# Layer 0 of a four-layer image network: another written-out order of its steps

## The chip, the cores and the metric

The kernel runs on one core of one Trainium2 chip. The metric is the device time of one execution in microseconds (us). Three runs of the kernel before took 6542.04, 6547.03 and 6561.65 us; their median, 6547.03 us, is the time that the prediction is held against. The core has a matrix engine (TensorE, called PE in the profile, with its weight loads as PEld), a vector engine (VectorE, DVE), a scalar engine for activations (ScalarE, ACT), a general engine (GpSimd, POOL), and a queue that issues transfers (SyncE, SP). Each engine runs its own list of instructions in order and waits where it needs a result of another.

## The reference

A batch of 32 images with 96 channels of 56x56 passes through four layers. Each layer is `x = x + layer(group_norm(x))`, with groups of three channels. Only layer 0 is touched by the change:

```python
h = einsum('nchw,oc->nohw', xn, w_exp)          # 96 -> 576 channels
h = silu(bn1(h))
h = depthwise_conv3x3(h, w_dw)                  # one 3x3 filter per channel
h = silu(bn2(h))
s = sigmoid(silu(h.mean((2, 3)) @ w_se1.T) @ w_se2.T)   # a gate per image and channel
h = einsum('nchw,oc->nohw', h * s[:, :, None, None], w_proj)   # 576 -> 96
out = bn3(h) + xn                               # and x + out outside
```

Layers 1 to 3 (a wavelet convolution, a quantised block of the same shape as layer 0, and a 9x9 convolution) follow one after the other.

## The kernel before, in words

**Tiling.** Layer 0 handles one image after the other. The 576 middle channels are cut into five blocks of 128 (the last is 64 channels, held twice). Blocks 0 and 1 have their 3x3 filters on VectorE, nine taps each; the upper half of block 2 is filtered on VectorE too; the lower half of block 2, all of block 3 and all of block 4 are filtered on TensorE, as matrix products with diagonal 32x32 weights.

**The steps.** A step has a letter, and its digits are its arguments: `e` (`expand`) multiplies one row tile of one block and lets ScalarE write it into a padded buffer (`e40` is block 4, tile 0); `f` (`first_tap`, ScalarE) and `t` (`tap`, VectorE) filter blocks 0 to 2 (`t18` is block 1, tap 8); `x0`, `a0`, `a1` and `c0` are the four filter groups on TensorE, each a call of `parts` with 9 taps x 4 x 4 small products on 32x32 parts of the array; `z` (`end_block`, ScalarE) ends a block; `g0` to `g4` make the gate (totals, squeeze, excite, gates, gated weights); `p` (`project`) multiplies one tile down to 96 channels; `d` (`add`, VectorE) adds it to the image; `o` (`store`) takes the statistics for the next layer and issues the stores; `s u m q v w b n r` are the group norm and the residual.

**Order.** `L0_ORDER` (line 61) is the list of the steps of one iteration n, and `run_steps` (line 116) goes through it once for each image. `-` after a step means image n-1 and `+` image n+1, so three images are in work at once. TensorE, VectorE and ScalarE keep the order of this list (line 473), each its own steps of it; the queue SP isn't among them, and has its transfers in the order in which they are written, each starting when what it waits for is done.

**Stores.** Two images share a buffer of the pool `pairs`, of which there are two. `store` of an odd image (line 453) issues six stores of the pair, 392 KB each and one per 16 channels (line 162), then the load of the pair after the next into the same buffer (`fetch(b + 3)`, line 211), and then some small copies for later layers (`aside`, lines 552 and 579).

**Buffers.** All products land in tiles of one PSUM pool with four buffers, taken in turn. A filter group takes two of them and gives them back after four ScalarE instructions. The normalised image `xn` has one buffer. Blocks 0, 1 and 2 share two padded buffers, block 3 and block 4 have one each.

Of the kernel before, what the change touches and what calls it, by code (L numbers as in the profile page):

```python
# [58 lines left out]
MANUAL = {mybir.EngineType.PE, mybir.EngineType.DVE, mybir.EngineType.Activation}  # L59
MANUAL_SP = MANUAL | {mybir.EngineType.SP}  # L60
L0_ORDER = """
    g2- g3- e40 t01 g4- e12 t02 t03 e30 t04 e41 e13 p0- d0- p1- s+ u+ t05 p2- m+ r t06 d1- t07 d2-
    p3- q+ f1 t08 e42 d3- e31 e32 e33 e20 v+ e21 o- w+ t11 e22 e23 t12 b+ e43 f2 t13 t14 t21 t15 z0
    x0 t16 a0 t22 t17 t18 n+ c0 t23 z1 t24 t25 t26 a1 t27 e00+ t28 z2 e01+ e02+ g0 e03+ g1 f0+ e10+
    e11+
"""
L2_ORDER = """
    e00 e10 e11 e12 l3 j0- d0- e01 e20 e02 e21 r u+ e03 e13 j1- m0 e22 d1- e30 m1 e40 v+ j2- d2- e31
# [1334 lines left out]
```

## Time and profile before

The profile is of one execution that took 6533.3 us; the span from its first to its last instruction is 6531.3 us. It is 13.7 us below the median of the runs.

| what | value | where it stands |
|---|---|---|
| median of the runs | 6547.03 us | times |
| profiled execution, span | 6533.3 us, 6531.3 us | times, page |
| TensorE busy | 5997.0 us, 92% | page, part 1 |
| VectorE busy | 4809.6 us, 74% | page, part 1 |
| ScalarE busy | 3988.3 us, 61% | page, part 1 |
| mean granted TensorE clock | 0.959 | clock of the core |
| filter groups of layer 0 on TensorE (line 376) | 875.6 us + 315.8 us busy | page, part 5 |
| idle before them, mostly for "issue" | 122.9 us + 110.0 us | page, part 5 |

In a profile a line such as `L376 PE MATMUL psd<-hpad,diag` means: line 376 of the kernel, on TensorE, matrix products that read the tiles hpad and diag and write psd. What stands behind "idle before" is how long the engine had nothing running before instructions of this group, and what ended that. "Issue" means that nothing in the profile was being waited for. The chain of waits goes back from the last instruction, at each step to what released it. A timeline lists one engine's instructions in order: start, length, what, and in brackets the idle time before.

The steps of layer 0 stand between about 30 us and 3,390 us of the span.

### The profile page before, as it was taken

The page shows a single profiled execution, that of the slowest core. Times are in us where ns is not written, and L with a number is a line of the kernel's source. Part 1 is how long each engine was busy: PE and PEld are TensorE (multiplying, and loading weights), DVE is VectorE, ACT ScalarE, POOL GpSimd, SP SyncE. Part 2 cuts the span into 40 slices and gives each one's busy share as a digit, 9 for nine tenths or more (in the row PEclk, how much of TensorE's full clock was granted, in tenths as well). Part 3 has the DMA queues.
Part 4 walks back from the last instruction along what each step waited for, and adds up shares of the span by engine and source line. Part 5 has one row for each costly group of instructions (what it writes and reads, how often), then busy time and mean ns, then how long its engine had stood idle before and what let it go on. Part 6 is the DMA issues. An engine that isn't in the chain of part 4 may idle for free.

```text
span 6531.3 us, 163776 instructions
## 1 busy us (share of the span) xinstructions
PE 5997.0 (92%) x72872; PEld 3871.0 (59%) x72872; DVE 4809.6 (74%) x5766; ACT 3988.3 (61%) x5716; POOL 230.5 (4%) x157
## 2 busy tenths in 40 slices
PE   6899999989899989998979999989899999999799
PEld 4555555555555555555545666668777777777344
DVE  7877778777787878777756766657677776676587
ACT  5566565655666565665635656657676776666455
POOL 4000000000000000000000000000000000000000
PEclk8999999999999999999989999989999999999899
DMA  3202221122212222122144676665869696962988
GB/s 99 34 22 53 53 44 32 41 55 49 41 27 47 54 46 41 26 48 41 17 48 134 148 141 158 148 47 38 52 39 53 40 54 40 52 37 30 167 257 243
DMA packets 1305952, 456.47 MB, mean 70 GB/s; under 512 B 1123150, under 2 KB 1301062, under 8 KB 1303326
## 3 DMA queue, kind: packets, MB, share of 16 engines
q1 hardware_dynamic: 1305246, 446.00, 45.6%
q8 instruction: 572, 9.37, 0.6%
q14 instruction: 134, 1.10, 0.1%
HBM read 284.90 MB, written 214.08 MB: 76 GB/s over the span
## 4 chain that ended last, share of the span: by engine, by line
PE 77%; DVE 9%; ACT 7%; issue 5%; DMA 1%; SPq 1%; POOL 0%; ACTq 0%; DVEq 0%
PE ps L329 11%; PE psd L376 11%; PE psd L1051 11%; PE psj L438 7%; PE ps L1032 6%; PE pc L1203 6%; PE pc L767 6%; DVE h L354 6%; PE psj L1088 3%; DVE h2c L354 3%; PE psj L442 3%; PE psj L443 3%; ACT hi L1004 2%; PE pc L751 2%; ACT a L1022 2%
## 5 line engine op out<-in xcount | busy, mean ns | idle before, releaser
L354 DVE SCALAR_TENSOR_TENSOR h<-hpad,l_wdw,h 128x3136 f32<-128x3136 f32 x512 | 1780.7, 3478 | 8.6 <-ACT h L349 1.7
L1051 PE MATMUL psd<-apad,diag 64*64 64x392 bf16 x20736 | 929.9, 331 | 117.2 <-issue 62.7
L376 PE MATMUL psd<-hpad,diag 32*32 32x392 f32 x27648 | 875.6, 543 | 122.9 <-issue 122.6
L329 PE MATMUL ps<-xn,l_wexp 96*128 96x392 f32 x2560 | 961.6, 533 | 16.7 <-DVE nm L296 6.2
L1051 PEld LDWEIGHTS <-diag 64*64 64x64 bf16 x20736 | 692.7, 107 | 350.2 <-issue 171.7
L376 PEld LDWEIGHTS psd<-hpad,diag 32*32 32x32 f32 x27648 | 556.8, 105 | 412.2 <-issue 267.2
L329 PEld LDWEIGHTS ps<-xn,l_wexp 96*128 96x128 f32 x2560 | 513.1, 205 | 405.4 <-issue 96.2
L597 ACT COPY T<-raw 32x112 f32<-32x112 f32 (+2 forms) x1440 | 462.8, 384 | 290.3 <-DMA raw<-tdiff 192.5
L1022 ACT ACTIVATE u<-ps,o,s 128x784 int16<-128x784 f32 x576 | 536.8, 1003 | 160.7 <-PE ps L1032 141.8
L1022 ACT ACTIVATE a<-psd,o,s 128x784 int16<-128x784 f32 x448 | 424.2, 1000 | 332.2 <-PE psd L1051 332.0
L341 ACT ACTIVATE hpad<-ps,o,s 128x784 f32<-128x784 f32 x512 | 537.3, 1071 | 82.5 <-PE ps L329 81.5
L354 DVE SCALAR_TENSOR_TENSOR h2c<-hpad,l_wdw,h2c 128x1568 f32<-128x1568 f32 x256 | 473.5, 1850 | 6.1 <-ACT h2c L349 0.4
L1032 PE MATMUL ps<-hi,l_w1q 96*128 96x392 f32 x1280 | 462.5, 361 | 9.3 <-ACT hi L1004 9.2
L1203 PE MATMUL pc<-x,T 128*112 128x416 f32 (+1 forms) x1152 | 414.8, 523 | 37.0 <-DMA X<-y 37.0
L767 PE MATMUL pc<-x,T 128*112 128x416 f32 (+1 forms) x1152 | 446.0, 523 | 0.0
L1032 PE MATMUL ps<-lo,l_w1q 96*128 96x392 f32 x1280 | 438.1, 342 | 0.0
L376 PE MATMUL psd<-hhalf,diag 32*32 32x392 f32 x9216 | 315.8, 555 | 110.0 <-issue 110.0
L360 ACT ACTIVATE hab<-psd,o,s 128x392 f32<-128x392 f32 x256 | 170.3, 674 | 396.8 <-PE psd L376 396.8
L438 PE MATMUL psj<-h,wg 128*96 128x392 f32 x1024 | 397.9, 509 | 2.3 <-DVE wg L429 2.3
L1203 PEld LDWEIGHTS pc<-x,T 128*112 128x112 f32 x1152 | 204.7, 178 | 246.6 <-issue 233.3
L349 ACT ACTIVATE h<-hpad,l_wdw 128x3136 f32<-128x3136 f32 x64 | 186.2, 2910 | 247.1 <-PE psj L438 247.1
L376 PEld LDWEIGHTS psd<-hhalf,diag 32*32 32x32 f32 x9216 | 191.7, 106 | 205.7 <-issue 158.5
(219 smaller groups left out, 8237.0 us busy)
## 6 DMA issues: line engine op xcount, KB each, us to landing
X<-y SPq DMA_DIRECT2D x192, 392.0 KB
y<-xt SPq DMA_DIRECT2D x180, 392.0 KB
xt<-in_x_dram SPq DMA_DIRECT2D x16, 2352.0 KB
y<-y SPq DMA_DIRECT2D x96, 392.0 KB
xt<-y SPq DMA_DIRECT2D x96, 392.0 KB
out_dram<-y SPq DMA_DIRECT2D x96, 392.0 KB
twav<-zwav SPq DMA_DIRECT2D x768, 36.8 KB
raw<-twav SPq DMA_DIRECT2D x96, 168.0 KB
```

Source lines behind the costliest of these rows:

```text
L329: nc.tensor.matmul(ps[:, j, :NT], wexp[:, k * 128 : k * 128 + 128], im["xn"][:, j, rows, :].rearrange("c h w -> c (h w)"), start=True, sto ...
L341: nc.scalar.activation(window(im["pad"][k][p], p.stop - (p.start or 0), 0, 0, r0, n).rearrange("p r (w j) -> p j r w", j=2), ps[p, :, :NT] ...
L354: nc.vector.scalar_tensor_tensor(h2, window(im["pad"][k], 128, t // 3 - 1, t % 3 - 1, 0, h2.shape[1]), wdw[:, k, t : t + 1], h2, ALU.mult, ...
L376: nc.tensor.matmul(ps[s // 2][q, s % 2, :NT].rearrange("p (r w) -> p r w", w=W2), diag[p, k - XX, t, :], v[:, :, s % 2 : W : 2], start=(t ...
L438: nc.tensor.matmul(out.rearrange("c (r w) -> c r w", w=W2), wg[:, k, :], im["h2"][k][:, rows, j::2], start=(k == 0), stop=False)
L442: nc.tensor.matmul(out, wg[:, COL[AB] + s, :], hab[:, i, j], start=False, stop=False)
L597: nc.scalar.copy(to.rearrange("x t (p s) -> x t p s", p=NPH), v[:, k])
L767: nc.tensor.matmul(ps[:PH, to], st["T"][j][:, h, k, :], st["x"][:, j, h, of], start=False, stop=(n == NK - 1))
L1022: nc.scalar.activation(out, ps, AF.Identity, bias=o[:, c : c + 1], scale=s[:, c : c + 1])
L1032: nc.tensor.matmul(ps[:, j, :NT], w1[:, k * 128 : k * 128 + 128], im[part][:, r0 : r0 + RT, :].rearrange("c h w -> c (h w)"), start=(part ...
L1051: nc.tensor.matmul(ps[q, j, :NT].rearrange("p (r w) -> p r w", w=W), diag[p, k, t, :], v, start=(t == 0), stop=(t == 8))
L1203: nc.tensor.matmul(ps[:, :, to], st["T"][:, h, k, :], st["x"][:, h, :, of], start=(n == 0), stop=(n == NK - 1))
```

## The change

`L0_ORDER` alone changes. The list has the same 77 steps; `e11`, `e30`, `e31` and `e32` change the iteration in which they stand: `e11` from the end of iteration n-1 to the start of iteration n, the other three from iteration n to the end of iteration n-1. So each image still runs the same instructions, with other neighbours.

```diff
 L0_ORDER = """
-    g2- g3- e40 t01 g4- e12 t02 t03 e30 t04 e41 e13 p0- d0- p1- s+ u+ t05 p2- m+ r t06 d1- t07 d2-
-    p3- q+ f1 t08 e42 d3- e31 e32 e33 e20 v+ e21 o- w+ t11 e22 e23 t12 b+ e43 f2 t13 t14 t21 t15 z0
-    x0 t16 a0 t22 t17 t18 n+ c0 t23 z1 t24 t25 t26 a1 t27 e00+ t28 z2 e01+ e02+ g0 e03+ g1 f0+ e10+
-    e11+
+    e11 g2- g3- t01 e40 g4- e12 t02 e33 e13 s+ p0- t03 p1- t04 p2- p3- d0- t05 r u+ d1- t06 t07 d2-
+    d3- m+ t08 f1 q+ t11 t12 a0 e41 e42 e20 t13 e21 e43 e22 t14 v+ w+ t15 t16 b+ t17 e23 f2 z0 c0
+    n+ t21 x0 t18 z1 a1 o- t22 t23 t24 e00+ t25 e01+ t26 e30+ t27 t28 e02+ e03+ e31+ z2 e32+
+    e10+ g0 g1 f0+
 """
```

On TensorE alone the two lists read, one iteration long:

```
before: g2- e40 e12 e30 e41 e13 p0- p1- u+ p2- p3- e42 e31 e32 e33 e20 v+ e21 e22 e23 e43 x0 a0 c0 a1
        e00+ e01+ e02+ e03+ g1 e10+ e11+
after:  e11 g2- e40 e12 e33 e13 p0- p1- p2- p3- u+ a0 e41 e42 e20 e21 e43 e22 v+ e23 c0 x0 a1
        e00+ e01+ e30+ e02+ e03+ e31+ e32+ e10+ g1
```

On VectorE the statistics of `o-` move from right behind `d3-` to behind `t18`, and block 1's taps stand ahead of the half block's.

## The prediction

> **What bounds the kernel now.** I read the page's busy shares first.
>
> ```profile
> PE 5997.0 (92%) x72872; PEld 3871.0 (59%) x72872; DVE 4809.6 (74%) x5766; ACT 3988.3 (61%) x5716; POOL 230.5 (4%) x157
> ```
>
> TensorE leads. Next I took the starts of the statistics of each image (line 88) in the timeline as marks, one per iteration, and the busy times between them. The columns are the stretch, its length, and busy us of PE, PEld, DVE, ACT and POOL, the clock, DMA share and GB/s.
>
> ```profile
> 1008.50:1103.70 95.20, 94.49 (x1366) 55.94 (x1365) 81.53 (x60) 63.19 (x76) 3.63 (x1) 0.96 0.06 15
> 1103.70:1216.90 113.20, 100.41 (x1366) 56.19 (x1365) 81.55 (x61) 63.00 (x76) 3.63 (x1) 0.91 0.36 68
> ```
>
> The same 1366 products take 95.2 us and then 113.2 us, all through layer 0: the 15 long stretches have a mean of 112.3, the 15 short ones 95.2. The long one has the DMA traffic. TensorE sets the time of both; VectorE's 81.5 us fit into either. The chain of waits shows where the 18 us go:
>
> ```profile
> 1117.55 3.93 PE psd L376 x113
> 1121.48 1.46 issue
> 1122.94 3.88 PE psd L376 x121
> 1126.82 2.61 issue
> 1129.43 5.19 PE psd L376 x124
> 1134.61 2.04 issue
> ```
>
> Filter groups come in bursts with holes in which nothing is waited for. TensorE's timeline gives such a burst its full count:
>
> ```profile
> 1122.94 3.88 PE L376 MATMUL psd<-hpad,diag 32*32 32x392 f32 x128 [1.46 <-issue]
> ```
>
> 128 products and their 128 weight loads are 256 instructions: one block of instructions, used up in 3.8 us, and then a wait for the next. The queue called "instruction" moves 16 KB pieces; in the long stretches these start at about 14.3, 21, 28, 34.5, 41, 49.5 and 54 us after the pair's first store. SP's queue:
>
> ```profile
> 1100.02 34.49 SPq L162 DMA_DIRECT2D y<-xt  x6
> ...
> 1142.97 0.34 SPq L211 DMA_DIRECT2D xt<-in_x_dram  x1
> ```
>
> The stores run from 0 to 42 us after that mark and the load of the next pair from 43 to 56, so one instruction block gets through per store (6.5 us), one during the load. Without stores the four groups took 33.3 us (1015.24 to 1048.5, 8.3 each); here 51.9.
>
> **What starts the stores.** In layer 0 the last add `d3-` and the statistics are neighbours; layer 2 has the same store function with work between them:
>
> ```profile
> 4774.85 1.15 DVE L1095 SCALAR_TENSOR_TENSOR xt<-psj,s,xt 96x392 f32<-96x392 f32 x2
> 4777.50 0.98 DVE L1041 TENSOR_SCALAR apad<-u 128x3136 bf16<-128x3136 int16 x1 [1.50 <-ACT u L1022]
> 4778.39 1.96 DVE L87 BATCH_NORM_STATS2 sth<-xt 96x6 f32<-96x392 f32 x4
> ```
>
> and, on SP,
>
> ```profile
> 4776.03 34.53 SPq L162 DMA_DIRECT2D y<-xt  x6
> ```
>
> The store starts 0.03 us after the last add ends (4776.00) and 2.4 us ahead of the statistics. So it follows `d3-`, wherever `o-` stands.
>
> [...] here the first hole comes after 170 to 240 products of a group, so the trace speaks for two blocks. [...] Here half-clock pieces of 3.4 or 6.8 us stand in most short stretches about 52 us in, right behind the squeeze and excite products: a mean loss of 3.4 us by the trace's record of the clock.
>
> **The change, part by part.** Nothing is added or removed: the same 77 steps, transfers included. Three things move.
>
> *(1) The undisturbed iteration.* Durations from the stretch at 1003 to 1099: expand tile 1.32 us (20 products in 6.59), project tile 6.78 (27.1 for four), excite 2.97, squeeze 0.66, tap 3.48, half tap 1.87, add 1.40, statistics 4.2, group eviction 2.7. I count from the end of `t28`. `z2` on ScalarE ends at 1.9, totals at 2.25, squeeze at 2.95; behind two evictions of 1.0 the squeeze's activation is done at 4.15; excite at 7.1, the gate's adds at 7.4, `t01` at 10.8, gated weights at 12.4. TensorE fills 7.1 to 12.4 with `e40 e12 e33 e13`, projects until 39.5; `d3-` ends at 40.9. From there VectorE runs without a wait: `t08` 3.45, `t11`-`t14` 13.9, `t15`-`t17` 10.4, `t21` 1.8, `t18` 3.4, `o-` 4.2, seven half taps 13.1, small ones 0.5: 50.7, so the next `t28` ends at 91.6. TensorE: `a0` 8.3, seven expands and `v+` 9.4, three groups 25.0, eight expands 10.6: 92.8, which is 1.2 before the totals release the squeeze. The iteration is 91.6, plus 3.4 of half clock 95.0, against 95.2. No gain, no loss. The cover is thin: VectorE and TensorE have 1 to 2 us to spare at `p0`, `d3-` and `g1`. Of what is queued behind new waits: PSUM tiles for `a0` need `d1-` and `d2-`, done at 37.5, 2 us early; ScalarE, where `f1` waits for `p3-` with `q+` and `a0`'s evictions behind it, is free at 45.5 and `a0` ends at 47.9; `n+` needs `b+` at 65.8 and gets its turn at 68.4. `e11` at the front is evicted at 8.3, before its buffer is needed. `o-` ends at 78.8, 38 us after the stores' start, before they end, so the load of the next pair (it overwrites what `o-` reads) isn't held.
>
> *(2) The storing iteration (15 of them).* In the new order stores start at `d3-`, 1.4 us after `a0` begins. After the mark at 40.9: `a0` from -1.4 to 6.9, `c0 x0 a1` from 16.5 to 41.5 if undisturbed. Both are in the window of 0 to 56; before, the groups stood at 10.5 to 43.8, undisturbed. I count blocks: a group needs 576 instructions, 2.25 blocks of 3.7 us; half a block and a full one are at hand at a start after slow work; the next are usable about 1.7 us after the starts above (16, 22.7, 29.5, 36, 42.7, 52.5, then free). Before, nine blocks from 10.5: 1.5 at hand, holes at 19.7, 26.4, 33.2, 39.7 and 46.4, end 61.8; the trace has 62.4, a loss of 18.0. After: `a0` has 1.5 of its 2.25 at hand and the third was asked for at about 0.5, before the queues fill: done at 7. While seven expands run (70 instructions in 9.2 us), the next block comes in. `c0` then starts at 16.5 with 1.5 blocks, gets a block at 22.7, and needs the next at 26, 33, 40 and 46; they come at 29.5, 36, 42.7 and 52.5: 6.75 blocks end at 56 to 57, a loss of 15.6. If `a0` asks later than 1 us, it waits for the turn at 7.5 and ends at 10 to 11; if `c0` then misses the turn at 21, the end is 60 to 61, a loss of 19.6. The phase of the block at the start decides, and the counts don't fix it. The first case gives 18.0 - 15.8 = 2.2 us per storing iteration, 33 us over 15; the second costs 1.6, 24 us.
>
> *(3) Squeeze and excite* have one expand tile between them, not two, and a wait of 1.2 us ahead. [...] short stretches lose 0 to 6.8 us now. I take +0.3 us for 31 iterations, 9 us; none as the low end, 3.4 in every second iteration, 53 us, as the high.
>
> Sum: -33 + 9 = -24 on the profiled 6533.3 us, 6509; the median is 13.7 above that execution, so 6523 us. Filling the pipeline differs too (three expands earlier, `e11` later), by a few us at one iteration in 33, either way; I leave it out.
>
> **The rivals.** *Even out* (6550 us): half of the storing iterations miss a turn, (-2.2 + 1.6) / 2 x 15 = -5, with the 9 us above +4. For it: four groups in the window now, where the last one used to run half outside it; against: two starts with full blocks, not one. *Slower* (6600 us): the half-clock piece of (3). No gain from blocks and 3.4 us in every second iteration is +53. It decides from six extra pieces of 6.8 us on (20 us). For it: 3 of 15 short stretches already have 13.7 us at half clock; [...] *The store is held back to `o-`* (6285 us): then the window would open behind `a1` and close before the next `a0`, and 15 x 17.5 = 262 us would go. Layer 2's start, 0.03 us behind the add, speaks against it.
>
> **How the numbers follow.** 0.3% of the time, 20 us, is what a measurement tells from none (the three runs lie 20 us apart). The gain by blocks has 0.37, evening out 0.33, slower 0.26, the held store 0.04. Faster is 0.37 + 0.04 = 0.41, same 0.33, slower 0.26. The likeliest case's own range is 6490 to 6527; the range with the others goes from 6470 (one hole of about 5 us less in each storing iteration, 75 us, and no extra half clock) to 6590, and leaves out the held store and the end of the slower case.
>
> **What would show it.** Right: long stretches of about 110.5, short of 95; stores starting within 0.1 us of `d3-`; in the storing iterations `a0` with at most one hole, and holes in `x0` and `a1`, with the end of `a1` 57 to 58 us after the first store. Wrong: long stretches below 105 (the stores start later, or blocks come faster), an end of `a1` past 61, half-clock pieces in more places than behind the excite, or TensorE waiting over 2 us for the totals or for gated weights in short stretches, which would make (1) wrong.

## The result and the profile after

The changed kernel takes 6571.55 us (median of 12 runs, 6548.36 to 6588.71) beside 6549.6 us of the kernel before in the same 12 rounds (6527.86 to 6582.35). The ratio is 1.0024, 95% interval [1.0005, 1.0043]. The forecast was 24 us faster. By the ratio it came out about 16 us slower, by the medians 22. That is about the 20 us (0.3%) that the prediction took for no change, but the interval leaves 1 out: there is a small loss and not a gain. The profiled execution took 6588.7 us, its span is 6586.6 us, the mean granted clock is 0.951 (0.959 before).

The two profiled executions are 55 us apart while the medians differ by 22: that of before lies 16 us below its median of 12, that of after 17 above. A second profile of the changed kernel is used below. Of the kernel before there is only the one, so differences to it are uncertain by its 16 us; the timed runs, split by their clocks under "The sum again", settle what the profiles can't.

From the page of the kernel after, part 1 and the groups of layer 0 on TensorE (busy time and mean ns | idle before, and what ended it):

```profile
PE 6061.0 (92%) x72872; PEld 3877.2 (59%) x72872; DVE 4807.8 (73%) x5766; ACT 3976.9 (60%) x5716; POOL 244.2 (4%) x157
...
L376 PE MATMUL psd<-hpad,diag 32*32 32x392 f32 x27648 | 898.3, 557 | 178.9 <-issue 175.2
...
L329 PE MATMUL ps<-xn,l_wexp 96*128 96x392 f32 x2560 | 986.8, 544 | 36.6 <-ACT hab L360 22.6
...
L376 PE MATMUL psd<-hhalf,diag 32*32 32x392 f32 x9216 | 291.7, 523 | 25.7 <-issue 24.9
```

The holes ahead of the filter groups fell from 122.9 + 110.0 = 232.9 us to 178.9 + 25.7 = 204.6: 28 us less, near the 33 us of the forecast. But the same instructions got longer: TensorE's busy time rose by 64.0 us, of which 25.2 are the expand tiles' (961.6 to 986.8). Most of this is a lower clock: by the trace's record of it, half clock took 267 us of the span before and 320 after. And a new wait of 22.6 us for `hab` stands in the list, once in the whole run.

To place these I cut both traces at the first projection `p0-` of each iteration. The columns are as in the prediction: stretch, length, busy PE, PEld, DVE, ACT, POOL, clock, DMA share, GB/s. Before, the start and one short and one long iteration:

```profile
0.00:146.60 146.60, 94.73 (x1332) 59.65 (x1333) 105.74 (x298) 87.91 (x97) 76.29 (x60) 0.88 0.39 106
976.00:1071.20 95.20, 94.49 (x1365) 55.96 (x1364) 82.89 (x62) 63.13 (x77) 3.63 (x1) 0.96 0.10 31
1071.20:1184.40 113.20, 100.41 (x1366) 56.18 (x1365) 81.07 (x61) 63.06 (x77) 3.63 (x1) 0.91 0.33 56
```

After:

```profile
0.00:163.30 163.30, 96.43 (x1340) 57.59 (x1341) 106.00 (x298) 89.83 (x99) 88.16 (x60) 0.83 0.36 97
996.90:1092.30 95.40, 95.16 (x1365) 56.88 (x1364) 82.38 (x61) 62.66 (x76) 3.69 (x1) 0.96 0.10 30
1092.30:1208.50 116.20, 102.35 (x1366) 58.54 (x1365) 81.54 (x61) 62.96 (x77) 3.63 (x1) 0.90 0.33 56
```

Three readings. The start is 16.7 us longer. The short iteration is the same. The storing iteration is longer at a lower clock. Over the 14 storing and 14 other iterations of images 1 to 28 (worked out from the trace; "half-clock loss" is half of the time that TensorE spent at half clock, idle or busy):

| kernel | storing: length | holes in groups | half-clock loss | other: length | half-clock loss | first projection at | last projection's start |
|---|---|---|---|---|---|---|---|
| before | 112.75 | 15.05 | 7.31 | 95.23 | 3.41 | 146.6 | 3353.6 |
| after | 114.36 | 13.44 | 9.87 | 95.76 | 3.66 | 163.3 | 3403.0 |
| after, second profile | 114.00 | 13.49 | 9.14 | 95.16 | 3.41 | 163.9 | 3387.8 |

So both profiles agree: holes fall by 1.6 us in each storing iteration, half-clock loss rises by 1.8 to 2.6 in the same iterations, and the iteration becomes 1.3 to 1.6 us longer than in the one profile of before, instead of 2.2 shorter. Behind layer 0 the rest of the span is 3177.7 us before, 3183.6 and 3189.1 after; with the same instructions there, this is scatter.

**What starts the stores, and what a late `a0` costs.** From the timelines of the kernel after, VectorE's and SP's, in one storing iteration:

```profile
1119.50 1.41 DVE L449 SCALAR_TENSOR_TENSOR xt<-psj,sc,xt 96x196 f32<-96x196 f32 x4 [3.78 <-PE psj L443]
...
1159.32 3.83 DVE L87 BATCH_NORM_STATS2 stt<-xt 96x6 f32<-96x392 f32 x8
```

```profile
1120.98 33.49 SPq L162 DMA_DIRECT2D y<-xt  x6
```

The last add ends at 1120.91, the store starts at 1120.98, the statistics come 38 us later. The chain of waits of the same iteration, from the start of `a0`:

```profile
1119.55 7.52 PE psd L376 x243
1127.07 4.49 issue
1131.56 1.59 PE psd L376 x24
1133.15 10.24 PE ps L329 x24
```

Here `a0` missed the turn: a hole of 4.49 us after 243 products. It is the case for which the prediction put the end of `a0` at 10 to 11 us; here it is 12.2 us after the last add. In the DMA packets of the same trace no 16 KB piece of the instruction queue starts between 1115.63 and 1129.09; the latter has landed at 1130.0, 1.6 us before TensorE goes on. Right behind the hole 24 expand products take 10.24 us where 24 take 8.11 elsewhere (a line of the third experiment below): TensorE runs at half clock from 1130.6, 1.0 us before the hole ends, to 1137.4, 6.8 us in all. The prediction had looked for such pieces at the squeeze and excite alone. The groups themselves are hardly slower: their busy time is 1191.4 us before and 1190.0 after.

**The start.** In iteration 0, `a0` now is the first step that writes `hab`. The timeline of ScalarE, after:

```profile
99.91 0.68 ACT L360 ACTIVATE hab<-psd,o,s 128x392 f32<-128x392 f32 x1 [21.03 <-DMA zdiff<-zt]
```

and the chain of waits there:

```profile
71.47 22.43 POOL zt L1160 x16
...
93.91 5.74 DMA zdiff<-zt
...
99.91 0.36 ACT hab L360
...
101.39 8.11 PE ps L329 x16
```

`hab` lies in a pool (`late`, line 261) whose memory held the tables that are built at the start and stored to `zdiff`. Its first write waits for that store. The eviction stands at the front of ScalarE's queue, TensorE runs out of PSUM tiles behind it (the 22.6 us of the page), and VectorE waits for a small product that TensorE does later:

```profile
109.62 0.15 DVE L300 TENSOR_SCALAR ve<-pn 96x1 f32<-96x1 f32 x1 [16.43 <-PE pn L292]
```

Before the change the wait for the same store fell to `h2c`, and cost ScalarE 6.04 us:

```profile
91.48 1.60 ACT L349 ACTIVATE h2c<-hpad,l_wdw 128x1568 f32<-128x1568 f32 x1 [6.04 <-DMA zdiff<-zt]
```

### The profile page after: what moved, and what is told of

Same layout as the page of the kernel before. It is cut to its first block, busy times and chain, and to the rows that moved or that the text cites. A ratio compares the mean times of both kernels' runs of the same rounds, so it can differ in the third digit from the quotient of the medians.

```text
span 6586.6 us, 163839 instructions
## 1 busy us (share of the span) xinstructions
PE 6061.0 (92%) x72872; PEld 3877.2 (59%) x72872; DVE 4807.8 (73%) x5766; ACT 3976.9 (60%) x5716; POOL 244.2 (4%) x157
## 4 chain that ended last, share of the span: by engine, by line
PE 81%; ACT 6%; issue 6%; DVE 3%; DMA 2%; POOL 1%; SPq 1%; POOLq 0%; ACTq 0%; DVEq 0%
PE psd L376 16%; PE ps L329 12%; PE psd L1051 10%; PE psj L438 7%; PE pc L767 6%; PE ps L1032 6%; PE pc L1203 6%; PE psj L1088 3%; PE psj L442 3%; PE psj L443 3%; DVE h L354 2%; ACT hi L1004 2%; PE pg L420 2%; PE pc L751 2%; ACT a L1022 2%
## 5 line engine op out<-in xcount | busy, mean ns | idle before, releaser
L376 PE MATMUL psd<-hpad,diag 32*32 32x392 f32 x27648 | 898.3, 557 | 178.9 <-issue 175.2
L1051 PE MATMUL psd<-apad,diag 64*64 64x392 bf16 x20736 | 925.1, 330 | 116.2 <-issue 63.7
L329 PE MATMUL ps<-xn,l_wexp 96*128 96x392 f32 x2560 | 986.8, 544 | 36.6 <-ACT hab L360 22.6
L376 PE MATMUL psd<-hhalf,diag 32*32 32x392 f32 x9216 | 291.7, 523 | 25.7 <-issue 24.9
L449 DVE SCALAR_TENSOR_TENSOR xt<-psj,sc,xt 96x196 f32<-96x196 f32 x512 | 179.5, 410 | 184.8 <-PE psj L443 184.6
```

Source lines behind the costliest of these rows:

```text
L329: nc.tensor.matmul(ps[:, j, :NT], wexp[:, k * 128 : k * 128 + 128], im["xn"][:, j, rows, :].rearrange("c h w -> c (h w)"), start=True, sto ...
L376: nc.tensor.matmul(ps[s // 2][q, s % 2, :NT].rearrange("p (r w) -> p r w", w=W2), diag[p, k - XX, t, :], v[:, :, s % 2 : W : 2], start=(t ...
L1051: nc.tensor.matmul(ps[q, j, :NT].rearrange("p (r w) -> p r w", w=W), diag[p, k, t, :], v, start=(t == 0), stop=(t == 8))
```

## The experiments

The theory (A) behind them: the 16 us are a start that is some 15 us later for `hab`, plus half-clock pieces in the storing iterations that eat what the blocks give; the length of the storing iterations as such comes from the stores' lying over the filter groups. The rivals (B) are named in each expectation. All ratios are to the kernel before, timed beside it. None of these kernels leaves out a computation.

**e1: `hab` outside the reused memory.**

```diff
     h2s = [cp.tile([128, H, W], F32, tag=f"h2{i}", name=f"h2{i}") for i in range(2)]
+    hab = cp.tile([128, NP, 2, NT], F32, tag="hab", name="hab")
...
-    hab = late.tile([128, NP, 2, NT], F32, tag="hab", name="hab")
```

> The changed kernel with the output tile of block 3 (hab) in memory that the tables of the later layers never used. Theory A (a part of the loss is one wait at the start: a0's first eviction stands in ScalarE's queue until the tables' last store has landed): the first projection starts at 146 to 151 us, not at 163.3; the later iterations stay at about 114 (with stores) and 96 us (without); the whole is 12 to 17 us shorter than the changed kernel, a ratio to the kernel before of 0.999 to 1.001. Theory B (the new order is slower in every iteration, the start is no matter): the first projection stays at 158 us or later, or the ratio stays at 1.002 or above.

Measured: 0.9978 [0.9969, 0.9986], 6539.28 us. The first projection stands at 149.0, as A expected; the ratio lies below A's 0.999 to 1.001. ScalarE's timeline of this kernel:

```profile
78.54 0.66 ACT L360 ACTIVATE hab<-psd,o,s 128x392 f32<-128x392 f32 x1
...
106.09 1.60 ACT L349 ACTIVATE h2c<-hpad,l_wdw 128x1568 f32<-128x1568 f32 x1 [15.13 <-DMA zdiff<-zt]
```

The wait has moved to `h2c` and is 15.13 us long. TensorE needs less of what stands behind it: it waits 6.1 us there, for the evictions of `hc`, where it waited 22.6 for `hab`. In the list of TensorE's waits up to the first projection:

```profile
PE psd L376 <- ACT hc L360: 6.1, 1, 6.1
```

So the wait for the store at the front of ScalarE's queue is shown to be the cause of the late start. The gain is larger than the start: against the second timing of the changed kernel (1.0028, below) the ratio is 0.0050 lower, some 33 us, of which the start is 15. The trace has 0.5 us less in each of the other iterations (94.66 against 95.16), 8 us in all. The two intervals allow 18 to 48 us, so the 23 us that the trace accounts for lie within them. Whether there is more isn't settled: the two kernels were timed on different chips, each beside the kernel before, and the edit also moves the other tiles of the pool `late`, which no run tests by itself.

**e2: the stores held until the statistics of `o-`.** A product by 1.0 on one column of the pair behind the statistics makes the stores wait for `o-`. It stands for the rival "the store is held back".

```diff
     def store(im):
         b = im["b"]
         channel_stats(nc, sm, im["xt"], mv_all[:, b, :], "t")
+        if b % 2 and b < B - 1:
+            v = im["xt"][:, 0, 0:1]
+            nc.vector.tensor_scalar(v, v, 1.0, None, ALU.mult)
         store_images(nc, y0, im)
```

> The changed kernel, in which one small multiplication by 1.0 on VectorE behind the statistics of an odd image touches the pair, so that the stores start behind o- and not behind d3-. Theory A (the stores take the turns of the instruction blocks): the holes in the filter groups of a storing iteration fall from 13.4 us to 4 or less, its half-clock loss from 9.9 to 4 to 6, and the iteration from 114 to 96 to 100 us; the load of the next pair then lands some 20 us after s+ would start, which costs the iteration behind it 3 to 5 us (99 to 101, not 96). Ratio to the kernel before 0.965 to 0.975. Theory B (the groups are too rich in instructions at any time, or the order has its own waits): holes of 10 us or more stay, ratio 1.000 to 1.005; or s+ costs all that is gained: the iteration behind takes 110 us or more.

Measured: 0.9657 [0.9639, 0.9676], 6329.43 us: 223 us less. The busy times of one storing iteration and the next, cut as above:

```profile
836.80:931.50 94.70, 94.16 (x1365) 57.48 (x1364) 82.42 (x62) 62.82 (x76) 3.69 (x1) 0.96 0.18 26
931.50:1030.60 99.10, 95.93 (x1366) 54.93 (x1365) 81.70 (x61) 62.43 (x76) 3.69 (x1) 0.97 0.29 68
```

The storing iteration has the length of the others; holes in the groups have a mean of 0.06 us. The 16 KB pieces of the instruction queue show the turns: in the groups of this iteration they start 3.5 to 3.7 us apart (886.61 to 900.74), in those of the changed kernel, under the stores, 6.5 to 9.0 us apart (1141.66 to 1171.17). The price is in the next one, since the load of the next pair starts later. SP's and ScalarE's timelines:

```profile
902.88 33.56 SPq L162 DMA_DIRECT2D y<-xt  x6
...
944.70 0.34 SPq L211 DMA_DIRECT2D xt<-in_x_dram  x1
```

```profile
957.73 2.82 ACT L287 ACTIVATE junk<-xt 96x3136 bf16<-96x3136 f32 x1 [24.92 <-DMA xt<-in_x_dram]
```

`s+` waits 24.92 us for the load; TensorE feels 2 to 3 us of it (these iterations are 98.06 on average). All is a little better than A had it; the storing iterations average 94.61 with a half-clock loss of 3.05. What follows: the 18 us of a long iteration come from the place of the stores, and nearly all of them can be had. It takes a store that waits for more than `d3-`, which the changed order alone doesn't do.

**e3: `a0` back among the other groups.**

```diff
-    d3- m+ t08 f1 q+ t11 t12 a0 e41 e42 e20 t13 e21 e43 e22 t14 v+ w+ t15 t16 b+ t17 e23 f2 z0 c0
-    n+ t21 x0 t18 z1 a1 o- t22 t23 t24 e00+ t25 e01+ t26 e30+ t27 t28 e02+ e03+ e31+ z2 e32+
+    d3- m+ t08 f1 q+ t11 t12 e41 e42 e20 t13 e21 e43 e22 t14 v+ w+ t15 t16 b+ t17 e23 f2 z0 c0
+    n+ t21 x0 t18 z1 a0 a1 o- t22 t23 t24 e00+ t25 e01+ t26 e30+ t27 t28 e02+ e03+ e31+ z2 e32+
```

> The changed kernel with a0 back beside the other groups: c0 x0 a0 a1 in a row. Theory A (blocks are counted against the turns that the stores leave, and a0 by itself brings about one more block of its own stock): the end of a1 is 62 to 64 us after the first store, not 61.0; the storing iteration is 114 to 116 us with holes of 14 to 16 us; the half-clock pieces 38 us into some iterations are gone; the first projection is back at 147 to 150 us, so the ratio to the kernel before is 1.000 to 1.003. Theory B (setting a0 apart, at the start of the stores, is what costs): storing iterations of 110 to 112 us, ratio 0.993 to 0.997.

Measured: 1.0075 [1.0056, 1.0094], 6601.96 us. The direction is as A has it, the ratio and the start are not. The storing iteration has 116.29 us with holes of 15.38, as much as before the change (15.05), and the other ones are 95.54. So setting `a0` apart is what took some 2 us of holes out of each storing iteration. The higher ratio has another part: expand tiles wait for the evictions of `hhalf` and `hpad`, 24.9 us in all of layer 0, where the second profile of the changed kernel has 1.2. The half-clock loss that stood 30 to 46 us after the mark, behind `a0`, falls from 1.10 to 1.46 us to 0.37. The first projection comes at 155.7, not at 147 to 150: TensorE's waits there are

```profile
PE ps L329 <- DVE nm L296: 14.0, 1, 14.0
...
PE psd L376 <- ACT hc L360: 6.4, 1, 6.4
```

The second is the same store again: `h2c` waits for it at the front of ScalarE's queue, and the evictions of `hc` stand behind it. It is in e1 too (6.1 us); what sets e3 back beside e1's 149.0 is mostly the first, which is 9.2 us there.

```profile
ACT h2c L349 <- DMA zdiff<-zt: 16.3, 1, 16.3
```

And a line of its chain of waits, behind 9.8 us of products without a hole, is the undisturbed price of 24 expand products used above:

```profile
1193.34 8.11 PE ps L329 x24
```

**e4 and e9: two expand tiles between squeeze and excite again.** e9 is the same kernel as e4, timed.

```diff
-    e11 g2- g3- t01 e40 g4- e12 t02 e33 e13 s+ p0- t03 p1- t04 p2- p3- d0- t05 r u+ d1- t06 t07 d2-
+    e11 e40 g2- g3- t01 g4- e12 t02 e33 e13 s+ p0- t03 p1- t04 p2- p3- d0- t05 r u+ d1- t06 t07 d2-
```

> The changed kernel with two expand tiles between squeeze and excite, as in the kernel before, and three behind. Theory A (the sparser stretch there costs clock, and the chain squeeze, excite, gate, projection has no slack): the half-clock loss behind the excite falls from 2.9 to about 1.9 us in storing iterations; the projection waits 1.0 to 1.5 us for the gated weights in the others, which grow from 95.8 to 96.5 to 97.5 us. Theory B (the clock pieces don't depend on it, the chain has slack): clock loss 9 to 10 us as before in storing iterations, and 95.5 to 96 us in the others.

> The changed kernel with two expand tiles between squeeze and excite, timed. Theory A (the spot between squeeze and excite costs clock in every iteration): about 1 to 1.5 us less than the changed kernel in each of 31 iterations, a ratio to the kernel before of 0.995 to 0.999, with the start still at 161 to 163 us. Theory B (the single look was a fast execution): 1.001 to 1.004.

Measured: e4 6529.94 us, a single time; e9 0.9985 [0.9973, 0.9996], 6545.78 us. The half-clock loss of the other iterations falls to 2.56 in both (3.41 and 3.66 without the edit), that of the storing ones to 7.56 and 7.44 (9.14 and 9.87). The wait of 1 to 1.5 us at the projection that e4's expectation added is 0.07 and 0.15 us: these iterations take 94.29 and 94.59, so the chain from excite to projection had the slack. The first projection of e9 is at 158.3, earlier than the 161 expected.

**e8: the changed kernel once more**, on the same chip and in the same rounds as e9.

> The changed kernel once more, for a second profile. Theory A (its three terms are of the kernel and not of one execution): first projection at 161 to 165 us; holes of a storing iteration 12.5 to 14.5 us, below 15.05 of the kernel before; storing iteration 113 to 115.5, the others 95 to 96.3; ratio 1.001 to 1.005. Theory B (the profile of the changed kernel was a slow execution): storing iterations 111 to 113, the others 94.5 to 95, with only the start as before.

Measured: 1.0028 [1.0014, 1.0042], 6573.21 us. The start, the holes and the iterations are as A has them (the table above). The intervals of e8 and e9 don't meet: one tile's place between squeeze and excite is worth 0.0043, 28 us. The clocks of the timed runs ("The sum again") have 38 us less of half clock in e9 and 8 us more of the rest; e9's trace has 13 us less of half clock in 15 undisturbed iterations and some 25 in 15 storing ones against e8's.

**e11: e1 and e4 together**, to see whether the two gains add up.

> The changed kernel with hab in memory of its own and two expand tiles between squeeze and excite, stores as in the change. Theory A (the start and the sparse spot are what turned a small gain into a small loss, and are separate): 1.0028 less 0.0022 to 0.0050 and less 0.0043, a ratio to the kernel before of 0.993 to 0.997; first projection 147 to 150 us, storing iterations 112 to 113.5, the others 93.5 to 95. Theory B (either alone does the same as both): 0.9975 to 0.999.

Measured: 0.9977 [0.9967, 0.9986], 6525.44 us (6542.65 before). They don't, as its B has it: 0.9978 with `hab` alone, 0.9985 with the tile alone, 0.9977 with both, on three chips, each beside the kernel before. In e11's trace the start is early (149.6) and the other iterations lose 2.80 us to the half clock, but the storing ones 9.26, no less than in the changed kernel. So what the tile's place costs is shown for the undisturbed iterations; how much it costs in the storing ones with an early `hab` isn't settled.

**e6 and e7: held stores with other orders.** In e6 the order of before gets held stores (a step `k`: the product by 1.0, the stores and the load, apart from the statistics), with the sums of the next image later; in e7 the changed order gets the same, `hab` as in e1 and the tile as in e4. e6, in the list of before:

```diff
-    g2- g3- e40 t01 g4- e12 t02 t03 e30 t04 e41 e13 p0- d0- p1- s+ u+ t05 p2- m+ r t06 d1- t07 d2-
-    p3- q+ f1 t08 e42 d3- e31 e32 e33 e20 v+ e21 o- w+ t11 e22 e23 t12 b+ e43 f2 t13 t14 t21 t15 z0
-    x0 t16 a0 t22 t17 t18 n+ c0 t23 z1 t24 t25 t26 a1 t27 e00+ t28 z2 e01+ e02+ g0 e03+ g1 f0+ e10+
-    e11+
+    g2- g3- e40 t01 g4- e12 t02 t03 e30 t04 e41 e13 p0- d0- p1- t05 p2- r t06 d1- t07 d2- p3- f1 t08
+    e42 d3- e31 e32 e33 e20 e21 o- t11 e22 e23 t12 e43 f2 t13 t14 t21 t15 z0 s+ x0 u+ m+ t16 q+ a0 v+
+    t22 t17 w+ t18 b+ n+ c0 t23 z1 t24 t25 t26 a1 t27 k- e00+ t28 z2 e01+ e02+ g0 e03+ g1 f0+ e10+ e11+
```

and e7, in the list of after:

```diff
-    e11 g2- g3- t01 e40 g4- e12 t02 e33 e13 s+ p0- t03 p1- t04 p2- p3- d0- t05 r u+ d1- t06 t07 d2-
-    d3- m+ t08 f1 q+ t11 t12 a0 e41 e42 e20 t13 e21 e43 e22 t14 v+ w+ t15 t16 b+ t17 e23 f2 z0 c0
-    n+ t21 x0 t18 z1 a1 o- t22 t23 t24 e00+ t25 e01+ t26 e30+ t27 t28 e02+ e03+ e31+ z2 e32+
+    e11 e40 g2- g3- t01 g4- e12 t02 e33 e13 p0- t03 p1- t04 p2- p3- d0- t05 r d1- t06 t07 d2-
+    d3- t08 f1 s+ t11 t12 a0 u+ m+ e41 e42 q+ e20 t13 e21 e43 e22 t14 e23 v+ w+ t15 t16 b+ t17 f2 z0 c0
+    n+ t21 x0 t18 z1 a1 o- k- t22 t23 t24 e00+ t25 e01+ t26 e30+ t27 t28 e02+ e03+ e31+ z2 e32+
```

> The order before, with the stores of a pair in a step of their own (k-) behind t27, where the last filter group ends, released by the same small multiplication; the norm of image n+1 (s u m q v w b) moves behind the projections, since its image now lands later. Theory A (the time of the stores, not the order of the steps, makes the long iterations): both kinds of iteration take 94 to 97 us, the holes in the filter groups of storing iterations fall from 15.05 us to below 2; ratio to the kernel before 0.957 to 0.967. Theory B (the new order is what gained in the run with held stores): storing iterations stay above 105 us, or the load lands after s+ and the other iterations grow by as much; ratio above 0.98.

> The changed kernel with the stores held behind o-, hab in memory of its own, two expand tiles between squeeze and excite, and s+ u+ m+ q+ behind the projections, so that nothing waits for the late load. Theory A (the costs are separate: turns of the blocks, the start, the half clock, the late load): storing iterations 93 to 95 us, the others 94 to 96, first projection 147 to 151 us, ratio 0.953 to 0.961, which is below 0.9657 of the run with held stores alone. Theory B (they are one cost seen from several sides): 0.963 or above.

Measured: e6 0.9703 [0.9675, 0.9731], 6364.23 us; e7 0.9695 [0.9666, 0.9723], 6351.46 us. Both are well below the kernel before and both miss what A expected; e7 lies where its B has it (0.963 or above). Later sums spare `s+` its wait for the load and bring a wait of their own: in one iteration of each, TensorE waits 3.1 us (e6) and 1.8 us (e7) for `nm`, the mean that `m` works out from the late sums.

e6 says more than its number: with the old order of the filter groups and held stores the mean iteration is 97.53 us (104 before, the mean of 112.75 and 95.23). So the long iterations come from when the stores run, not from the order of the groups.

**e10: the best version**, the edits of e1, e2 and e4 together.

> The changed kernel with the stores held behind o-, hab in memory of its own, and two expand tiles between squeeze and excite; s+ stays where the change has it. Theory A (the three costs are separate): 0.9657 of the held stores less about 14 us of the start and 0.5 to 1 us of half clock in each of 31 iterations, that is 0.958 to 0.963; storing iterations 93 to 94.5 us, those behind them 96.5 to 98, first projection 147 to 150 us. Theory B (they don't add up, as in the run with late sums): 0.9645 to 0.970.

Measured: 0.9625 [0.9605, 0.9644], 6288.93 us beside 6542.65: 254 us less, as expected. A storing iteration and the next one:

```profile
1010.00:1104.80 94.80, 94.21 (x1366) 57.11 (x1365) 83.15 (x62) 62.55 (x77) 3.69 (x1) 0.96 0.19 27
1104.80:1201.50 96.70, 93.92 (x1365) 55.32 (x1364) 80.12 (x61) 62.41 (x76) 3.69 (x1) 0.98 0.30 69
```

What is left of the load's lateness is a wait of the small product of the late sums (tile `pn`, 1.7 us in the second stretch); the mean of such iterations is 97.17, that of the storing ones 94.67.

## Why the prediction was wrong

The forecast of -24 us was the sum of -33 for the blocks, +9 for the squeeze and 0 for the start. The start failed most plainly: 0 was said, 17 us measured. The half clock was sized too small and looked for at one place only: 9 us said, some 25 measured in the iterations. The blocks gave less than said: some 22 us for 33 (both worked out under "The sum again"). By its own steps:

**(1) The undisturbed iteration: right.** 95.0 was said, 95.2 to 95.8 measured, 95.23 before. The waits of over 2 us for totals or gated weights that would have shown it wrong didn't come (0.1 to 0.3 us of other idle time in each), and e9's 94.59 shows the chain less thin than I wrote. The prediction put the wait of the squeeze for the totals at 1.2 us; it is 0.2.

**(2) The blocks: the mechanism right, the likeliest case half the truth.** The stores start 0.07 to 0.08 us behind `d3-`. In the traces, all holes over 0.3 us in the filter groups of the 14 storing iterations (80 before, 63 after) end 1.2 to 2.2 us behind the landing of a 16 KB piece, and where only filter products stand between two of them, these are 127 or 128 (once 256). Holes fall by 1.6 us for each storing iteration. I had said that "the phase of the block at the start decides, and the counts don't fix it": 6 of 14 `a0` have a hole (2.9 to 4.7 us), 8 have none. The last product of `a1` ends 63.7 us after the first store in the 6 and 59.9 in the 8, 61.5 over all (60.8 in the second profile), against 57 to 58 said for the better case, 60 to 61 for the worse and 63.6 before. So both cases were put some 2 to 3 us too early, and the better one is the case in 8 of 14. (The step's 2.2 us also takes 15.8 off 18.0 where its count has 15.6, 3 us over 15 iterations.)

What failed is that the step took the better case for all iterations, and that it counted holes as lost time and nothing behind them. A late `a0` also brings a half-clock piece over the expand tiles that follow: by place, the storing iterations lose 1.10 to 1.46 us 30 to 46 us after the mark, where before they lost none. Half-clock pieces away from the excite, and an end of `a1` past 61, were among the prediction's own signs of being wrong.

**(3) Squeeze and excite: the sign right, the size too small.** 0.3 us for each iteration, 9 us, was taken between bounds of 0 and 53. That one tile less there costs half clock was the author's estimate; the runs show it by this one edit: undoing it is worth 28 us (e9 against e8), with 38 us less of half clock by the clocks of the timed runs. Beside the profile of before, the loss isn't seen in the undisturbed iterations (3.41 and 3.66 beside 3.41), which are half of those in which the prediction counted it; near the excite in the storing ones it is 2.93 and 3.29 beside 1.95, 15 to 20 us over 15. e11 keeps the price from being closed.

**The start: the term that was left out.** "Filling the pipeline differs too ... by a few us ... either way; I leave it out." It was 16.7 and 17.3 us in the two profiles, two thirds of the forecast gain and most of the measured difference, and e1 takes 15 of it back by one edit that has nothing to do with steady iterations. The step missed that moving `a0` ahead makes it the first writer of a tile in reused memory. In the trace of before, the wait for `zdiff` at `h2c` (6.04 us) was to be seen.

**The sum again.** Each timed run has its span and its mean clock, and (1 - clock) x span is taken for what half clock took of it (the records of the profiles before and after hold no clock but full and half, and with their clocks unrounded it gives their 267 and 320 us). The mean of this over the runs of a kernel, and the mean of the rest, against the kernel before beside it (27 or 36 runs), in us:

| kernel | runs | half clock, against before | rest, against before |
|---|---|---|---|
| changed (e8) | 17 | +35 | -15 |
| tile back (e9) | 20 | -4 | -8 |
| `hab` elsewhere (e1) | 22 | 0 | -14 |
| both (e11) | 22 | -13 | -2 |
| stores held (e2) | 4 | -72 | -153 |
| held, with both (e10) | 5 | -89 | -158 |

The first four are good to about 6 us (two standard errors). In the profiles, the late start is 10 us of half clock, which pass while TensorE waits, and 7 of the rest. Taken off the first row, this leaves -22 of the rest, near the 28 us of holes that went, and +25 of half clock. So the sum -33 + 9 + 0 came out as -22 + 25 + 17 = 20. How the 25 split between the holes behind `a0` and the excite is known from the profiles alone: 17 to 22 us and 15 to 20, beside a profile of before with 267 us of half clock, where its timed runs have means of 278 to 293 on three chips.

Added up from the profiles, the start (17), the storing iterations (15 x 1.3 to 1.6) and the other ones (15 x -0.1 to 0.5) come to 35 to 49. The execution of before lies 16 us below its median and the two of the changed kernel 6 and 17 above theirs; with both taken off, 13 to 16 are left, and the medians say 20 to 22.

What stays open is e1: by its clocks it has no more half clock than the kernel before beside it, though its trace shows nearly as much in the storing iterations as the changed kernel's (9.02 beside 9.14 and 9.87). The 15 us of the start are shown; the rest of its 33 us is not explained.

**The rivals:** nearest is "even out" (6550 us), for more reasons than its own: in it half of the storing iterations were to miss a turn, which is nearly so (6 of 14), but the start and the half clock made the rest. "The store is held back" was refused for the right reason, and e2, where it is built, gives 6329 for the 6285 worked out; the iterations that wait for the load (98.06 instead of 95.2, 15 of them, 43 us) and the late start (17 us) more than make up the difference. The slower one's half clock is there, at other places too, and at about half of its price of 53 us.

## What to carry to other kernels

When an order of steps is changed, walk through the first iteration by itself: ask which step now is the first to write each tile in reused memory and what stands behind it in its engine's queue. Where an engine is fed by instruction blocks, count transfers that overlap dense groups first, since moving the stores out of that time was worth 243 us (0.9657 against 1.0028) where the order of the groups within it moved 1 to 2 us of holes for each storing iteration; count for a hole both its length and the half-clock time behind it (2.9 to 4.7 us and up to another 1.7 to 5.1 in the holes behind `a0`). And split the timed runs by their clocks before you explain the iterations of one profile: here that told a lost clock from a lost turn, where two profiles were 55 us apart.

## What the runs showed of the hardware

**POOL's long copies end where a tap of VectorE ends.** The same 16 copies at the start, from POOL's timelines before, after and in e1:

```profile
72.09 12.78 POOL L1160 COPY zt<-rev 96x27 f32<-96x27 f32 x16
```

```profile
71.47 22.42 POOL L1160 COPY zt<-rev 96x27 f32<-96x27 f32 x16
```

```profile
71.22 28.85 POOL L1160 COPY zt<-rev 96x27 f32<-96x27 f32 x16
```

(Most of the 16 are smaller than the shape shown: 12 have 96x18.) They end at 84.9, 93.9 and 100.1. One copy takes from 0.20 to 3.46 us; a tap takes 3.48. VectorE's taps (`h<-hpad,l_wdw,h`) run, with small instructions between them, until 83.5, 93.2 and 100.0:

```profile
76.56 6.99 DVE L354 SCALAR_TENSOR_TENSOR h<-hpad,l_wdw,h 128x3136 f32<-128x3136 f32 x2
```

```profile
75.75 17.44 DVE L354 SCALAR_TENSOR_TENSOR h<-hpad,l_wdw,h 128x3136 f32<-128x3136 f32 x5
```

```profile
92.99 7.01 DVE L354 SCALAR_TENSOR_TENSOR h<-hpad,l_wdw,h 128x3136 f32<-128x3136 f32 x2
```

In all three the copies end 0.1 to 1.3 us after a run of taps does. Copy by copy, in the traces before and after: each one that is under way when a tap ends (4 of the 16 before, 7 after) takes 0.80 to 3.46 us and ends 0.07 to 0.08 us behind that tap; the others take 0.20 to 0.21 us. What holds a copy there isn't shown. If the taps do, this also feeds back on the start: VectorE has five taps in a row from 75.75 after and two from 76.56 before, and the copies end 9.0 us later, and with them the tables, whose store the first write to `hab` waits for.

**The holes behind `a0` cost twice.** All six behind `a0` in the profile after (2.9 to 4.7 us) are followed by a piece at half clock: one of 3.4 us, four of 6.8 and one of 10.2, so up to another 1.7 to 5.1 us of TensorE's time (in some the first microsecond lies in the hole). None of the eight iterations without the hole has one there.

**An undisturbed iteration is 91.9 us and what half clock takes.** In the kernel before, cut at the starts of line 88, the short stretches are 91.9 us long with no half clock, 93.6 where it took 1.7, 95.2 or 95.3 where it took 3.4, and 98.5 where it took 6.8; the last one alone, 96.1 with 6.8, is out of line.
